# Doing the last layer's block endings inside its edge loop, at places given by limits

## The chip, the cores and the metric

One core of one Trainium2 chip. The metric is the device time of one execution in microseconds (us), median of several.

The engines go by their short names: in this kernel PE does the matrix products, DVE (vector engine) the sums and one-hots, ACT (scalar engine) the relu, POOL (GpSimd) issues the gathers, and SP issues plain loads and stores. SBUF and PSUM are the two memories in which the kernel has its tiles; the matrix products go to PSUM. A line of a timeline gives start and duration in us, engine, line of the kernel, operation, and what it writes and reads (out<-in); in brackets is the idle time of the engine before it and what ended that. A group line gives, behind its count (x), the busy time in us, the mean of one in ns, and the idle time before. The profile leaves numbers at the end of names out, so x3 is x there.

## The reference, cut to what matters

Four layers of a graph network on 4096 nodes of 512 features and 65536 edges, each added to its input. The last layer is a graph convolution with a linear map, a sum over edges and a relu:

```python
# layer 3; x is the result of layer 2 (the kernel calls it x3)
h = jnp.maximum(_layernorm(x, axis=-1), 0.0)
z = h @ W.T + b
out = jax.ops.segment_sum(norm[:, None] * z[row], col, num_segments=n)   # norm = dis[row] * dis[col]
x = x + jax.nn.relu(out)
```

`dst`, over which the last sum runs, is sorted and denser at low nodes (4096 u^2 with u uniform).

## The kernel before

The nodes are 32 blocks of 128. The edges are sorted by block and cut into tiles of 128; a block has a whole number of tiles, so that each tile adds to one block. The sums live in `acc`, 32 blocks of 128x512 in SBUF. The main part of the loop has 528 tiles; a branch holds up to 16 more, which these inputs do not need.

```python
def one_hots(pool, loc, t0, n):                         # which row of the block does each edge add to?
    oh = pool.tile([P, n, P], F32, name="oh")
    nc.vector.tensor_tensor(oh, row_i.unsqueeze(1).to_broadcast([P, n, P]),
                            loc[:, t0:t0 + n].unsqueeze(2).to_broadcast([P, n, P]), op=OP.is_equal)
    return oh

def add_to(b, ps):                                      # b is read from a table at run time
    into = acc[:, ds(b, 1), :D].rearrange("p b d -> p (b d)")
    nc.vector.tensor_add(into, into, ps)

# sum_edges: groups of U = 4 tiles, order of every engine fixed by hand
for i in range(-4, groups):
    if i + 4 < groups:
        g = got[i + 4] = ep.tile([P, U, D], F32, name="g", bufs=6)
        for j in range(U):
            gather(g[:, j, :], table, idx[:, t:t + 1])  # an indirect DMA, issued by POOL
    if 0 <= i + 1 < groups:
        ohs[i + 1] = one_hots(ep, loc, first + (i + 1) * U, U)
    # ... (nothing more for i < 0)
    for j in range(0, U, pair):
        # ... matmul of one-hots and gathered rows into PSUM
        add_to(block_of(nc.vector, bi, first + i * U + j), ps)

# ... layers 0 to 2, and the table ztab of layer 3 ...
in_two(1, TD_MAIN, TD, sum_edges(ztab, d_src, d_loc, bi_d, 1))     # main part, then a branch
with tc.tile_pool(name="l3_end", bufs=3) as lp:
    for b0 in range(0, NB, BG):                                    # BG = 4 blocks at a time
        xt = lp.tile([P, BG, D], F32, name="xt")
        nc.sync.dma_start(xt, blocks_of(x3, b0))
        for j in range(BG):
            b = b0 + j
            nc.scalar.activation(acc[:, b, :D], acc[:, b, :D], AF.Relu, scale=dis[:, b:b + 1])
            nc.vector.tensor_add(xt[:, j, :], xt[:, j, :], acc[:, b, :D])
        nc.sync.dma_start(blocks_of(out, b0), xt)
```

## Time and profile before

| | us |
|---|---|
| median, before | 6524.2 (6512.2 to 6527.4, 4 runs) |
| span of the profile | 6523.0 |
| last store of the table issued, to first gather of layer 3 | 3.95 |
| first to last gather of layer 3 | 661.0 |
| last gather to the end of the last sum | 5.9 |
| end of the last sum to the end of the program | 51.5 |

The table is read off the timeline. The prediction shows the lines that carry it. Three more are wanted, from the issue table of the kernel before: what goes where, from which queue, how many, how large, and the median time from issue to landing.

```profile
xt<-x SPq DMA_DIRECT2D x16, 1024.0 KB, 7.5
g<-ztab,d_src POOLq DMA_INDIRECT x528, 3.7
out_dram<-xt SPq DMA_DIRECT2D x8, 1024.0 KB, 4.9
```

### The profile page before, as it was taken

To read this page: it belongs to the slowest core of one execution; us is meant where nothing else is said; L and a number is where in the kernel's file an instruction comes from. 1 tells how busy PE (TensorE), PEld (TensorE's weight loads), DVE (VectorE), ACT (ScalarE), POOL (GpSimd) and SP (SyncE) were. 2 spreads that over 40 slices of the span, in tenths; PEclk is the share of its full clock that TensorE was granted. 3 is DMA by queue.
4 is the path that set the end of the run, shared out by engine and by line. 5 is a ranking of instruction groups with operands and counts; after the bars stand their busy time and mean duration, and the time that the engine had idled before them with its cause. 6 is when DMAs were issued, how large, how long until landed. Compare 5 with 4: busy or idle time off the path is not lost. (4 is left out here: it accounts for less than half of the span.)

```text
span 6523.0 us, 65629 instructions
## 1 busy us (share of the span) xinstructions
PE 5718.0 (88%) x18462; PEld 2778.4 (43%) x18462; DVE 4141.7 (63%) x7141; ACT 2937.3 (45%) x3977; POOL 3254.1 (50%) x3324
## 2 busy tenths in 40 slices
PE   6678887888779799999999999999999889978885
PEld 4366664322224344444444444444444365532221
DVE  7577778455443376676676776776766545556665
ACT  3244444300011277777777777777777533300001
POOL 1277772477760365555555555555555100037774
PEclk9899999999899899999999999999999899989998
DMA  8777775566774333333333333333333211137777
GB/s 225 182 220 214 218 215 176 162 201 203 195 214 175 125 109 103 102 98 104 101 98 105 101 98 102 103 98 106 100 98 104 82 45 62 59 106 209 210 209 243
DMA packets 399757, 926.39 MB, mean 142 GB/s; under 512 B 135926, under 2 KB 135926, under 8 KB 399382
## 3 DMA queue, kind: packets, MB, share of 16 engines
q0 software_dynamic: 230976, 721.66, 37.6%
q1 hardware_dynamic: 168406, 200.39, 9.6%
q8 instruction: 155, 2.54, 0.2%
q14 instruction: 220, 1.80, 0.1%
HBM read 818.71 MB, written 103.11 MB: 141 GB/s over the span
## 5 line engine op out<-in xcount | busy, mean ns | idle before, releaser
L438 PE MATMUL m_ps<-w_sb,h_t 128*128 128x512 f32 x4224 | 1905.9, 599 | 31.2 <-ACT h_t L957 31.2
L803 PE MATMUL sum_ps<-g,oh 128*128 128x512 f32 x2144 | 1146.9, 636 | 218.1 <-DMA g<-ztab,d_src 80.2
L438 PEld LDWEIGHTS m_ps<-w_sb,h_t 128*128 128x128 f32 x4224 | 771.1, 190 | 983.6 <-issue 791.2
L449 POOL DMA_INDIRECT qg<-qtab,eg x528 | 504.0, 954 | 990.6 <-ACT h_t L957 845.7
L449 POOL DMA_INDIRECT g<-ztab,d_src x528 | 501.4, 950 | 866.4 <-issue 811.6
L459 DVE TENSOR_TENSOR acc<-acc,sum_ps 128x512 f32 x800 | 550.2, 688 | 546.4 <-PE sum_ps L803 541.4
L803 PEld LDWEIGHTS sum_ps<-g,oh 128*128 128x128 f32 x2144 | 336.9, 191 | 1015.4 <-DVE acc L459 388.5
L449 POOL DMA_INDIRECT g<-ytab,s_dst x544 | 536.9, 987 | 353.2 <-DMA ytab<-acc 185.6
L914 POOL DMA_INDIRECT eg<-aug,d_eid x528 | 569.0, 1078 | 242.4 <-issue 131.0
L449 POOL DMA_INDIRECT rows<-htab,s_dst x544 | 585.9, 1077 | 204.9 <-issue 138.9
L957 ACT COPY h_t<-tr_ps 128x512 f32<-128x512 f32 x528 | 283.6, 589 | 777.6 <-PE tr_ps L955 777.6
L735 PE MATMUL sum_ps<-rows,oh 128*128 128x261 f32 x2176 | 551.5, 410 | 60.3 <-PE sum_ps L735 41.2
L449 POOL DMA_INDIRECT pg<-ptab,eg x528 | 508.7, 963 | 160.9 <-issue 160.6
L735 PEld LDWEIGHTS sum_ps<-rows,oh 128*128 128x128 f32 x2176 | 427.3, 202 | 163.3 <-PE sum_ps L735 66.3
L967 PE MATMUL small_ps<-z,oh 128*128 128x512 f32 x1056 | 477.8, 595 | 8.4 <-DVE z L1027 8.4
L1006 DVE TENSOR_TENSOR z<-m_ps,b_bc 128x512 f32<-128x512 f32 x132 | 91.3, 692 | 467.3 <-PE m_ps L438 467.3
L459 DVE TENSOR_TENSOR acc<-acc,small_ps 128x512 f32 x528 | 361.1, 684 | 31.8 <-PE small_ps L967 4.3
L1165 ACT ACTIVATE acc<-acc,dis 128x512 f32<-128x512 f32 x32 | 19.7, 706 | 671.2 <-DVEq L464 671.2
L1027 DVE TENSOR_TENSOR z<-z,t 128x1024 f32<-128x1024 f32 x264 | 310.4, 1217 | 8.2 <-ACTq L464 4.8
L992 DVE TENSOR_TENSOR z<-m_ps,b_bc 128x512 f32<-128x512 f32 x132 | 91.3, 692 | 352.6 <-PE m_ps L438 352.6
L967 PEld LDWEIGHTS small_ps<-z,oh 128*128 128x128 f32 x1056 | 201.5, 191 | 263.7 <-issue 221.9
L955 PEld LDWEIGHTS tr_ps<-ident,pg 128*128 128x128 f32 x2112 | 248.0, 142 | 151.1 <-issue 120.0
(248 smaller groups left out, 8389.5 us busy)
## 6 DMA issues: line engine op xcount, KB each, us to landing
aug<-row SPq DMA_DIRECT2D x32, 560.0 KB, 3.9
places<-loc_rows SPq DMA_DIRECT2D x68, 256.0 KB, 3.8
xt<-in_x_dram SPq DMA_DIRECT2D x16, 1024.0 KB, 5.7
row<-in_edge_attr_dram SPq DMA_DIRECT2D x32, 512.0 KB, 6.6
x<-xt SPq DMA_DIRECT2D x16, 1024.0 KB, 4.3
xt<-x SPq DMA_DIRECT2D x16, 1024.0 KB, 7.5
rows<-htab,s_dst POOLq DMA_INDIRECT x544, 3.8
g<-ytab,s_dst POOLq DMA_INDIRECT x544, 3.7
```

What stands on the lines that cost most here:

```text
L438: nc.tensor.matmul(ps, h_t[:, k, :], w_sb[:, k0 + k, :], start=start and k == 0, stop=stop and k == KC - 1)
L449: nc.gpsimd.indirect_dma_start(out=dst_ap, out_offset=None, in_=table, in_offset=bass.IndirectOffsetOnAxis(ap=idx, axis=0))
L459: nc.vector.tensor_add(into, into, ps)
L735: nc.tensor.matmul(ps[:, c, :HW], oh[:, j + k, :], rows[:, j + k, c * HW:(c + 1) * HW], start=k == 0, stop=k == 1)
L803: nc.tensor.matmul(ps, oh[:, j + k, :], g[:, j + k, :], start=k == 0, stop=k == pair - 1)
L914: nc.gpsimd.indirect_dma_start(out=eg[:, j // 2, (j % 2) * HALF:(j % 2 + 1) * HALF], out_offset=None, in_=aug.rearrange("e c -> (e c)").un ...
L955: nc.tensor.transpose(h_ps[:, k, :], h[:, j, k * P:(k + 1) * P], ident)
L957: nc.scalar.copy(h_t, h_ps)
L967: nc.tensor.matmul(ps, oh, m, start=True, stop=True)
L992: nc.vector.tensor_add(zz[:, 0, :], ps, b2_bc)
L1006: nc.vector.tensor_add(zz[:, 1, :], ps, b2_bc)
L1027: nc.vector.tensor_mul(mz[:, j:j + 2], mz[:, j:j + 2], t[:, j:j + 2])
```

## The change

Its intent is to take the ending off the end. Because the edges are sorted by block, a block's sums are complete long before the loop is. But where a block ends depends on the data, and the instruction order does not. So each block gets a limit, a tile after which it is taken to be complete: 230 + 10b for block b. A flag `late` is computed from the real ends; if a block ends behind its limit, a branch at the very end does all blocks over. ACT now writes to a tile of its own (`t_end`), not over `acc`, so that doing it over is possible.

```diff
+    LIMITS = ((32, 17), (230, 10))
 # ... in the sort, for each of the two orders o:
+        limit = pool.tile([1, NB], F32, name="limit")
+        nc.gpsimd.iota(limit, pattern=[[LIMITS[o][1], NB]], base=LIMITS[o][0], ...)
+        nc.vector.tensor_tensor(limit, til[:1, :], limit, op=OP.is_gt)
+        nc.vector.reduce_max(over, limit, axis=AX.X)
+        nc.vector.tensor_copy(late[:, o:o + 1], over)
 # ... in sum_edges, behind the four tiles of a group:
+                    if follow and first == 0:
+                        follow(first + (i + 1) * U)
 # ... the ending:
-    in_two(1, TD_MAIN, TD, sum_edges(ztab, d_src, d_loc, bi_d, 1))
-    with tc.tile_pool(name="l3_end", bufs=3) as lp:
-        # ... (the loop over blocks shown above)
+    class Ending:
+        def load(self, b):
+            if b < NB:
+                self.xs[b] = self.pool.tile([P, D], F32, name="x_end", bufs=self.ahead + 3)
+                nc.sync.dma_start(self.xs[b], x3[b * P:(b + 1) * P, :])
+        def follow(self, tiles):
+            self.finish()
+            while self.next < NB and tiles >= LIMITS[1][0] + LIMITS[1][1] * self.next:
+                self.begin()
+        def begin(self):
+            b, self.next = self.next, self.next + 1
+            t = self.pool.tile([P, D], F32, name="t_end", bufs=4)
+            nc.scalar.activation(t, acc[:, b, :D], AF.Relu, scale=dis[:, b:b + 1])
+            self.ready.append((b, t))
+        def finish(self):
+            for b, t in self.ready:
+                xt = self.xs.pop(b)
+                nc.vector.tensor_add(xt, xt, t)
+                nc.sync.dma_start(out[b * P:(b + 1) * P, :], xt)
+                self.load(b + self.ahead)
+            self.ready = []
+        # ... __init__ (six loads ahead), the_rest (what is left behind the loop)
+    with tc.tile_pool(name="l3_end", bufs=1) as lp:
+        ending = Ending(lp, 6)
+        sum_edges(ztab, d_src, d_loc, bi_d, 1, follow=ending.follow)(0, TD_MAIN)
+        ending.the_rest()
+    for flag in (more, late):
+        with tc.If(nc.values_load(flag[:, 1:2], min_val=0, max_val=1) > 0):
+            if flag is more:
+                sum_edges(ztab, d_src, d_loc, bi_d, 1)(TD_MAIN, TD)
+            with tc.tile_pool(name="l3_late", bufs=1) as lp:
+                Ending(lp, 6).the_rest()
```

More of the change, by code (lines that the diff above doesn't have):

```diff
@@ L97 @@
     more = keep_pool.tile([1, 2], I32, name="more")
+    late = keep_pool.tile([1, 2], I32, name="late")
     by_src = ctx.enter_context(ExitStack())
@@ L240, in by_order @@
         nc.vector.tensor_copy(more[:, o:o + 1], over)
+        limit = pool.tile([1, NB], F32, name="limit")
+        nc.gpsimd.iota(limit, pattern=[[LIMITS[o][1], NB]], base=LIMITS[o][0], channel_multiplier=0,
+                       allow_small_or_imprecise_dtypes=True)
+        nc.vector.tensor_tensor(limit, til[:1, :], limit, op=OP.is_gt)
+        nc.vector.reduce_max(over, limit, axis=AX.X)
+        nc.vector.tensor_copy(late[:, o:o + 1], over)
         tile_i = pool.tile([P, G], F32, name="tile_i")
@@ L773, with sum_edges @@
     l0_pool.close()
-    def sum_edges(table, idx, loc, bi, pair, beside=None):
+    def sum_edges(table, idx, loc, bi, pair, beside=None, follow=None):
         U = 4
@@ L1157, with __init__, the_rest @@
                     norm.rows(j, h3[p - 2][:, j, :], xt[:, j, :])
-    in_two(1, TD_MAIN, TD, sum_edges(ztab, d_src, d_loc, bi_d, 1))
-    with tc.tile_pool(name="l3_end", bufs=3) as lp:
-        for b0 in range(0, NB, BG):
-            xt = lp.tile([P, BG, D], F32, name="xt")
-            nc.sync.dma_start(xt, blocks_of(x3, b0))
-            for j in range(BG):
-                b = b0 + j
-                nc.scalar.activation(acc[:, b, :D], acc[:, b, :D], AF.Relu, scale=dis[:, b:b + 1])
-                nc.vector.tensor_add(xt[:, j, :], xt[:, j, :], acc[:, b, :D])
-            nc.sync.dma_start(blocks_of(out, b0), xt)
+    class Ending:
+        def __init__(self, pool, ahead):
+            self.pool, self.ahead, self.next, self.xs, self.ready = pool, ahead, 0, {}, []
+            for b in range(ahead):
+                self.load(b)
+        def load(self, b):
[18 more added lines that the diff above has]
+            self.ready = []
+        def the_rest(self):
+            self.finish()
+            while self.next < NB:
+                self.begin()
+                self.finish()
```

## The prediction

> **What bounds the kernel now.** The change touches only the last layer's loop over edges and what follows it, so I read that part. First the busy times by stretch (columns: stretch and its length, busy us and instruction counts of PE, weight loads, DVE, ACT, POOL, then granted clock, DMA share, GB/s). 5804 to 6466 is the loop, 6471 to 6523 the end.
>
> ```profile
> 5804.00:6178.00 374.00, 316.09 (x590) 89.96 (x590) 242.90 (x367) 0.00 (x0) 282.92 (x298) 0.99 0.71 208
> 6178.00:6466.00 288.00, 244.29 (x460) 70.59 (x460) 190.36 (x287) 0.00 (x0) 218.00 (x230) 0.99 0.71 210
> 6471.00:6523.00 52.00, 0.00 (x0) 0.00 (x0) 20.45 (x33) 19.70 (x32) 0.00 (x0) 0.52 0.90 323
> ```
>
> The loop uses 71% of the DMA engines, two thirds of DVE and none of ACT. The end uses the DMA engines at 90% and little else: two stretches with opposite limits, one behind the other. Next the chain that ended last: 0.319 of a window of 83 us is loads of x3 and 0.126 stores of the output.
>
> ```profile
> by line: DMA xt<-x 31.9%; DMA out_dram<-xt 12.6%; DVE xt L1166 8.3%; DVEq L1198 0.7%; issue 0.5%; SPq L1162 0.5%; DVEq L1166 0.2%
> ```
>
> Then the order in time where loop meets end, and at the last gather:
>
> ```profile
> 6465.57 0.95 POOL L449 DMA_INDIRECT g<-ztab,d_src  x1 [0.30 <-issue]
> ...
> 6470.78 0.69 DVE L459 TENSOR_TENSOR acc<-acc,sum_ps 128x512 f32 x1 [0.38 <-PE sum_ps L803]
> 6471.77 19.70 ACT L1165 ACTIVATE acc<-acc,dis 128x512 f32<-128x512 f32 x32 [671.21 <-DVEq L464]
> 6471.81 1.68 SPq L1162 DMA_DIRECT2D xt<-x  x3
> ...
> 6514.58 3.01 SPq L1167 DMA_DIRECT2D out_dram<-xt  x2
> ```
>
> The last sum ends at 6471.5 and the program at 6523.0: the end costs **51.5 us**, in which 8 MiB are loaded and 8 MiB stored, through three buffers. Last, who paces the loop: the groups of instructions of its steady part (5840 to 6466).
>
> ```profile
> L449 POOL DMA_INDIRECT g<-ztab,d_src x500 | 474.9, 950 | 152.3 <-issue 98.7 <-PE sum_ps L803 29.2 <-DMA g<-ztab,d_src 24.4
> L459 DVE TENSOR_TENSOR acc<-acc,sum_ps 128x512 f32 x500 | 343.8, 688 | 212.9 <-PE sum_ps L803 208.8 <-DVE acc L459 1.3
> L444 DVE TENSOR_TENSOR oh<-row_i,d_loc 128x512 f32<-128x512 f32 x124 | 84.9, 685 | 0.0
> ```
>
> POOL's idle time is 152.3 us before 500 gathers, 0.30 each, the same whatever it is put down to. So POOL runs without a stop, 0.95 + 0.30 = 1.25 us per gather, and 528 of them take 661 us (6465.57 - 5804.54). **Issuing the gathers is the bound**, PE and DVE follow. They land 3.7 us after issue, and a buffer of 24 tiles stands between, so small delays on PE or DVE are not felt by POOL.
>
> **What the Trainium skill says.** "Perfetto Trace Analysis", Optimization Strategy: where the contended engine changes over time, interleaving the regimes may help; the first fence is such a case. "DMA: Bandwidth & Descriptors", Issuing engines are not separate DMA queues: transfers of all issuers share the same 16 engines and interleave; so loads and stores put into the loop compete with the gathers, for which no run shows the price yet. "VectorE: DVE Perf Modes", The TRN2 errata: an fp32 add of N elements takes (N+151)/0.96 ns, 691 for 512; the trace has 687 to 688. "SBUF — State Buffer", SBUF: two separate sides: a DVE operation with two SBUF inputs shuts out a GpSimd operation that reads SBUF for its whole length. The trace agrees, and this matters here:
>
> ```profile
> 6195.64 0.68 DVE L444 TENSOR_TENSOR oh<-row_i,d_loc 128x512 f32<-128x512 f32 x1
> 6195.74 1.40 POOL L449 DMA_INDIRECT g<-ztab,d_src  x1 [0.30 <-issue]
> ...
> 6335.35 0.95 POOL L449 DMA_INDIRECT g<-ztab,d_src  x1 [0.30 <-DMA g<-ztab,d_src]
> 6335.86 0.69 DVE L444 TENSOR_TENSOR oh<-row_i,d_loc 128x512 f32<-128x512 f32 x1
> ```
>
> One-hots (two SBUF inputs) that run across a gather's start lengthen it: 1.40 instead of 0.95, about until the one-hots' end. The sums (one input in PSUM) start beside gathers all the time and lengthen none. In this loop one-hots mostly start 0.3 to 0.7 us after a gather starts, so they end before the next one, and only 8 of 528 gathers are over 1.0 us.
>
> **The change part by part.**
> 1. Removed: the end, 51.5 us.
> 2. Its work goes into the loop: block b is begun after tile 230 + 10b, rounded up to a group of 4. 520 is the last such number that is at most 528 (b = 29), so 30 blocks are done inside and two after. ACT has nothing else there. DVE gets 30 adds of 0.69 = 21 us in the 373 us of the last 298 tiles, where it idles a third, 125 us. ACT's read of a block holds back the next sum: in the layer before, such an ACT operation takes 0.72 and starts 0.04 after DVE; the one-hots (0.69) cover most of it. Nothing there reaches POOL through a buffer.
> 3. Are the limits kept? From the given edges I counted the tiles of each block: the last tile of every block lies 5 or more tiles within its limit (5 at blocks 19 to 24), the total is 527 of 528. So neither branch is taken and nothing is done twice.
> 4. Added end. After the last sum: ACT on block 30 (0.72), its add beside ACT on block 31, the second add, together about 2.2; a store of 256 KB, which lands in 2.0 to 2.5 in the issue table; about 1.5 for two branches and 0.9 for the closing of the program, as before. Sum **6.5 us**. Saved so far: 51.5 - 6.5 = 45.
> 5. Start of the loop. Nine loads of x3 now come beside the last store of ztab, which the first gather waits for (issued 5800.59, gather 5804.54). The order on the queue shows one load ahead of that store, eight just behind it: 2 MiB, some 6 us of the engines at the end's 323 GB/s. I charge **1.5**.
> 6. Shut-out. The order on DVE has each final add (two SBUF inputs) between a group's last sum and the one-hots after it. It takes the place of the one-hots, which is safe; but it pushes them back by 0.6, from 0.3-0.7 to 0.9-1.3 us of a 1.25 us cadence, that is, across the next gather's start. A lengthening of 0.2 to 0.45 then falls on POOL, the bound. 30 times 0.3 = **9 us** (an estimate from the fence above).
> 7. Limits: one iota and three DVE operations on 32 numbers in each of two sorts, some 0.15 us each: **0.7** at most.
>
> Sum: 45 - 1.5 - 9 - 0.7 = 34 us. From the median of 6524.5: **6490 us**, or 0.5% less.
>
> **Rivals.** (a) *Contention on the DMA engines sets the pace.* 55 transfers of 256 KB in 373 us are 39 GB/s. At the end's rate (0.90 for 323 GB/s) that is 0.11, and 0.71 becomes 0.82: room is left. Layer 0 speaks for it: a 256 KB load per 8 gathers, and gathers of 1077 ns on average. But there the long ones go with a DVE multiply of two SBUF inputs at the gather's start, and gathers beside the bulk of a load's packets have their 0.95. If it held all the same, 0.13 on 300 gathers would cost 39 us: the gain would be eaten, 6520. (b) *The adds shut out nothing*, since the phases shift or POOL has a reserve: 45 - 2 = 43 us, 6481. (c) *A block is late*, by a fault in my count: all 32 are redone behind the loop, 50 us or more: 6530 or above. (d) *DVE becomes the bound*: its share rises from 66% to about 72% in the second part, so no.
>
> **Range and chances.** (b) to a somewhat worse case of 6 gives 6478 to 6500; the three runs of before scatter by 15 us, so I widen to 6474 to 6506. 2% are 130 us, far more than the end that can be hidden, and more than any rival costs: within 2% with 0.98.
>
> **What would show it.** Right: the last sum to the end of the program 5 to 9 us; no instruction of either branch's body; POOL's gap before a gather still 0.30, but some 20 to 30 gathers of the last 298 at 1.1 to 1.45 us, each with one-hots across its start; loop from first to last gather 668 to 673 us; DMA share in the second part 0.80 to 0.84. Wrong: gathers lengthened where only loads or stores run (a), idle time of POOL above 0.30 (a buffer came late), fewer than 10 long gathers (b), or 32 more ACT operations after the loop (c). Any of these moves the time by its own term; the sign would turn only with (a) in full or (c).

## The result, and the profile after

6491.4 us (6483.5 to 6502.4, 4 runs) against 6524.2 us. The ratio is 0.9954, with a 95% interval from 0.9935 to 0.9974. (A ratio is the mean time of one kernel's fast runs over that of the other's of the same rounds, so not quite the ratio of the medians.) The change gains half a per cent. Executions over 1.5% slower than the fastest of the same kernel are left out of the means.

First the busy times by stretch of the changed kernel, with the columns of the prediction's first fence.

```profile
5803.00:6178.00 375.00, 310.64 (x586) 91.33 (x586) 244.44 (x371) 4.35 (x7) 284.62 (x297) 0.98 0.74 219
6178.00:6470.00 292.00, 231.62 (x453) 72.03 (x452) 201.46 (x306) 16.59 (x23) 223.40 (x225) 0.99 0.78 238
6470.00:6492.00 22.00, 9.48 (x19) 2.91 (x18) 9.30 (x14) 2.06 (x3) 5.83 (x6) 0.82 0.42 134
```

ACT now works inside the loop, and the DMA engines carry 238 GB/s where they carried 210. There are only 225 POOL operations in 292 us of the second stretch, that is 1.30 us each; before there were 230 in 288 us, 1.25 each. The loop has become slower. The end, from the timeline of the changed kernel:

```profile
6482.53 0.69 DVE L469 TENSOR_TENSOR acc<-acc,sum_ps 128x512 f32 x1 [1.60 <-PE sum_ps L813]
6483.31 1.33 ACT L1192 ACTIVATE t_end<-acc,dis 128x512 f32<-128x512 f32 x2 [10.22 <-DVE acc L469]
6484.07 1.30 DVE L1198 TENSOR_TENSOR x_end<-x_end,t_end 128x512 f32<-128x512 f32 x2 [0.85 <-ACT t_end L1192]
6484.78 0.94 SPq L1199 DMA_DIRECT2D out_dram<-x_end  x2
```

The last sum ends at 6483.2, two blocks are left, and the program ends at 6491.6: 8.4 us in place of 51.5. Where the time between went, by the same five stretches:

| stretch | before | after | difference |
|---|---|---|---|
| program start to the last store of the table | 5800.6 | 5798.0 | -2.6 |
| that store to the first gather | 3.95 | 4.81 | +0.9 |
| first to last gather | 661.0 | 673.7 | +12.7 |
| last gather to end of last sum | 5.9 | 6.7 | +0.8 |
| end of last sum to end of program | 51.5 | 8.4 | -43.1 |
| sum | 6523.0 | 6491.6 | -31.4 |

The first row is scatter: a second profile of each kernel, with nothing edited, had 5789.4 before and 5801.9 after (runs e10 and e11 below). Since the stages before the loop scatter by some 15 us (this row has 5787 to 5802 in the eleven profiles without an edit to layer 1, all but e7 and e9), more than what the experiments are about, I compare loops (first to last gather), and times only where the difference is larger.

The groups of instructions of the changed kernel, in the stretch from 6110 to 6460, in which endings run:

```profile
L459 POOL DMA_INDIRECT g<-ztab,d_src x271 | 268.8, 992 | 82.6 <-issue 71.6 <-DMA g<-ztab,d_src 5.8 <-PE sum_ps L813 5.2
L454 DVE TENSOR_TENSOR oh<-row_i,d_loc 128x512 f32<-128x512 f32 x67 | 46.0, 687 | 0.0
L1198 DVE TENSOR_TENSOR x_end<-x_end,t_end 128x512 f32<-128x512 f32 x27 | 18.6, 687 | 0.0
```

POOL's idle time is still 0.30 per gather (82.6 / 271). No buffer holds it up. The gathers themselves are longer, 992 ns on average where they had 950. Counted in the trace: of the last 298 gathers 44 are over 1.0 us (4 before), of the first 230 there are 6 (4 before). Each long one has one-hots or a final add across its start, as in this piece of the changed kernel's timeline:

```profile
6466.44 0.69 DVE L1198 TENSOR_TENSOR x_end<-x_end,t_end 128x512 f32<-128x512 f32 x1
6467.04 0.69 DVE L454 TENSOR_TENSOR oh<-row_i,d_loc 128x512 f32<-128x512 f32 x1
...
6467.27 1.27 POOL L459 DMA_INDIRECT g<-ztab,d_src  x1 [0.30 <-PE sum_ps L813]
```

The add takes the place of the one-hots, the one-hots slide to 6467.04, and the gather that starts at 6467.27 takes 1.27 us. It ends 0.81 us after the one-hots do; in the prediction's example the gather of 1.40 us ends 0.82 after them. Over the whole loop of the changed kernel 50 gathers are lengthened by over 0.05 us, 40 with one-hots and 10 with an add across their start, and every one ends 0.81 to 0.82 us after that operation does. One-hots that run only some 0.13 us or less into a gather lengthen nothing (0.95 = 0.13 + 0.82).

### The profile page after: what moved, and what is told of

It reads as the page before. It is cut to its first block, busy times and chain, and to the rows that moved or that the text cites. A ratio compares the mean times of both kernels' runs of the same rounds, so it can differ in the third digit from the quotient of the medians.

```text
span 6491.6 us, 65768 instructions
## 1 busy us (share of the span) xinstructions
PE 5700.9 (88%) x18462; PEld 2779.8 (43%) x18462; DVE 4140.9 (64%) x7147; ACT 2940.7 (45%) x3977; POOL 3264.9 (50%) x3326
## 5 line engine op out<-in xcount | busy, mean ns | idle before, releaser
L813 PE MATMUL sum_ps<-g,oh 128*128 128x512 f32 x2144 | 1133.7, 633 | 245.9 <-DMA g<-ztab,d_src 94.6
L1192 ACT ACTIVATE t_end<-acc,dis 128x512 f32<-128x512 f32 x32 | 23.0, 721 | 663.7 <-DVE acc L469 663.7
L979 PEld LDWEIGHTS small_ps<-z,oh 128*128 128x128 f32 x1056 | 201.5, 191 | 263.7 <-issue 221.9
```

The costliest lines, as they stand in the source:

```text
L813: nc.tensor.matmul(ps, oh[:, j + k, :], g[:, j + k, :], start=k == 0, stop=k == pair - 1)
L979: nc.tensor.matmul(ps, oh, m, start=True, stop=True)
```

## The experiments

**The theory** going in: the loop's 12.7 us are DVE operations with two SBUF inputs that run across the start of a gather and lengthen it (shut-out), because the final adds push the one-hots. **The rival**: the 16 MiB that now run on the DMA engines beside the gathers slow POOL or the gathers as such (contention). "Long" means over 1.0 us, counted among the last 298 gathers on the two digits that the timeline prints; e1, e8 and e10 have one more each if 1.002 to 1.005 us counts as long.

| run | loop, us | long | median, us (runs) |
|---|---|---|---|
| before; again (e10) | 661.0; 662.0 | 4; 6 | 6521.6 (8, the rounds of e6 to e8) |
| changed; again (e11) | 673.7; 672.9 | 44; 41 | 6491.4 (4, other rounds) |
| e1, adds in mid group | 667.5 | 23 | 6483.5 (4) |
| e2, transfers only | 670.9 | 35 | 6480.2 (4) |
| e3, ACT and adds only | 669.0 | 30 | 6487.1 (4) |
| e4, one-hots before the add | 672.6 | 46 | 6490.1 (4) |
| e5, ACT's result in PSUM | 668.4 | 24 | 6481.1 (1) |
| e6, and the one-hots' row | 658.8 | 0 | 6470.2 (4) |
| e7, combined version | 658.9 | 0 | 6458.7 (4) |
| e8, no branches | 672.4 | 42 | 6488.7 (4) |
| e9, kernel before with the row in PSUM | 658.7 | 0 | 6502.4 (4) |

In all of them but e6, e7 and e9 the first 230 gathers take 288.2 to 289.5 us, in those three 287.4 to 287.5: up to the first ending all loops with the same one-hots go alike.

### e1: the final adds in the middle of a group

```diff
                         side.step()
+                        if follow and first == 0 and j == 1:
+                            follow.__self__.finish()
                     if follow and first == 0:
                         follow(first + (i + 1) * U)
```

> Only the place of the final adds changes: after the second sum of a group instead of after its fourth. Shut-out theory: the add then lies 0.3 to 0.7 us after a gather's start, pushes no one-hots and crosses no gather's start. Of the last 298 gathers at most 12 are over 1.0 us (44 in the changed kernel), and first to last gather takes 661 to 664 us (673.7). Contention rival: transfers are the same, so 35 or more long gathers and 671 to 675 us.

Measured: 23 long gathers and 667.5 us. This lies between the two expectations: half of the loss goes, half stays. The place of the adds matters, with all transfers kept, which the rival cannot explain; but they are not all of it. Both expectations missed.

### e2: the transfers alone

```diff
-            t = self.pool.tile([P, D], F32, name="t_end", bufs=4)
-            nc.scalar.activation(t, acc[:, b, :D], AF.Relu, scale=dis[:, b:b + 1])
+            t = None
...
-                nc.vector.tensor_add(xt, xt, t)
+                nc.vector.memset(xt[:, 0:1], 0.0)
```

> The loads and stores of the ending stay in the loop, paced by a memset of one column on DVE; ACT operation and add are taken out (result wrong on purpose: x3 with a zeroed column). Shut-out theory: the memset has no SBUF input, so at most 15 of the last 298 gathers are over 1.0 us, loop 661 to 665 us. Contention rival: the transfers alone cost the 12 us, loop 671 to 675 us.

Measured (result wrong): 35 long gathers and 670.9 us. My theory missed here: with no add to push anything (the memset takes 0.06 us), most of the loss was there. The rival's range was met to 0.1 us. But every one of the long gathers again has one-hots across its start. What probably moved them shows in the waits of PE and in how long a gather takes to land, both from 6110 to 6460. The kernel before:

```profile
PE sum_ps L803 <- DMA g<-ztab,d_src: 45.2, 128, 2.0
DMA to landing us min/median/max: 3.4/3.6/5.5
```

Transfers only:

```profile
PE sum_ps L813 <- DMA g<-ztab,d_src: 65.0, 98, 1.6
DMA to landing us min/median/max: 3.5/4.2/5.6
```

The gathers land 0.6 us later in the median, and unevenly; PE waits 65 us for them, not 45. POOL keeps its own cadence, but sums and one-hots come behind the landings and slide against it. Counted from the trace over the last 72 one-hots of the loop: those that start less than 0.55 us before the next gather's start, so that they run over 0.13 us into it, are 6 in the kernel before, 34 in the changed one and 37 here (each to within 1, since the timeline has two digits). Starts at random in the cadence of 1.25 us would give 0.55 / 1.25 of 72, that is 32 (an estimate from these numbers): the kernel before has favourable places, the changed one and e2 about what chance gives. So I formed a second theory: *anything* that shifts DVE against POOL brings the shut-out, the pushing add and the late landing alike.

### e3: ACT and the adds alone

```diff
-            if b < NB:
+            if b >= self.ahead + 3 and b < NB:
+                self.xs[b] = self.xs[b - self.ahead - 3]
+            elif b < NB:
                 self.xs[b] = self.pool.tile([P, D], F32, name="x_end", bufs=self.ahead + 3)
...
-                nc.sync.dma_start(out[b * P:(b + 1) * P, :], xt)
+                if b >= NB - 2:
+                    nc.sync.dma_start(out[b * P:(b + 1) * P, :], xt)
```

> ACT operations and adds stay in the loop, loads beyond the first nine blocks and all stores but the last two are taken out (result wrong on purpose). Shut-out theory: 30 to 50 of the last 298 gathers over 1.0 us, loop 670 to 675 us as in the changed kernel. Contention rival: loop back at 661 to 664 us.

Measured (result wrong): 30 long gathers and 669.0 us, at the lower edge of the count and 1 us under the range of the theory, far from the rival's. Gathers land as before, in 3.7 us; 28 of 72 one-hots run across a start by the same count. So ACT and the adds alone cost 8 us and the transfers alone 10, and both together 12.7: not a sum, since a gather is lengthened once whatever moved the one-hots.

### e4: one-hots first, then the add

```diff
+                    if follow and first == 0 and i:
+                        follow(first + i * U)
                     g, oh = got.pop(i), ohs.pop(i)
...
-                    if follow and first == 0:
-                        follow(first + (i + 1) * U)
```

> The final add and the one-hots change places on DVE: one-hots first, the add behind them. Shut-out theory: the second of the two operations is the one that crosses a gather's start, whichever it is; so the count stays at 30 to 50 long gathers in the last 298 and the loop at 670 to 675 us, but now most long ones have the add across their start (10 of 50 in the changed kernel). A rival that only one-hots hurt: under 12 long gathers and 661 to 664 us.

Measured: 46 long gathers and 672.6 us, as expected of the theory; but of the 55 gathers of the whole loop that are lengthened by over 0.05 us only 15 have the add across their start, 41 the one-hots (one has both). The part of the expectation on which of the two it would be was wrong. That fits the second theory: the landings move the one-hots in any order.

### e5 and e6: nothing with two SBUF inputs

In e5 ACT writes `t_end` into PSUM; the add keeps its place and length. In e6 the row that the one-hots compare with is copied into PSUM once, too, before the loop.

```diff
+            self.tpool = pool                      # e5 and e6; then set to a pool in PSUM
-            t = self.pool.tile([P, D], F32, name="t_end", bufs=4)
+            t = self.tpool.tile([P, D], F32, name="t_end", bufs=2)
...
+                row = None                         # e6 alone
+                if follow:
+                    row = rps.tile([P, P], F32, name="row_ps")      # rps: a pool in PSUM
+                    nc.vector.tensor_copy(row, row_i)
-                        ohs[i + 1] = one_hots(ep, loc, first + (i + 1) * U, U)
+                        ohs[i + 1] = one_hots(ep, loc, first + (i + 1) * U, U, row)
```

> ACT writes its result into PSUM, so the final add has one SBUF input; its place and length are unchanged, and it still pushes the one-hots. Shut-out theory: the long gathers with the add across their start (10, 4.1 us in the changed kernel) vanish, those with the one-hots (40, 10.1 us) stay: loop 668 to 672 us. Rival that the adds themselves are the cost: 661 to 663 us. Contention rival: unchanged, 673 to 675 us.

> As the run before, and the row of numbers that the one-hots compare with lies in PSUM too, so no DVE operation of this loop has two SBUF inputs. Shut-out theory: no gather over 1.0 us at all in this loop, first to last 659 to 661.5 us, under the kernel before change (661.0). Contention rival: 35 or more long gathers in the last 298, 671 to 675 us.

Measured in e5: 668.4 us; no lengthened gather is left that has the add alone across its start, and in the whole loop 32 with one-hots remain (one of them has the add across its start too). As expected. In e6 none is long and the loop takes 658.8 us, 2 us less than before the change and 0.2 under the expected range. The groups of instructions of e6, then its gathers (shortest, median and longest in ns) and their landing, all from 6110 to 6460:

```profile
L459 POOL DMA_INDIRECT g<-ztab,d_src x277 | 261.9, 945 | 84.4 <-issue 69.8 <-DMA g<-ztab,d_src 7.9 <-PE sum_ps L818 6.7
L454 DVE TENSOR_TENSOR oh<-row_ps,d_loc 128x512 f32<-128x512 f32 x69 | 47.2, 684 | 0.0
L1204 DVE TENSOR_TENSOR x_end<-x_end,t_end 128x512 f32<-128x512 f32 x28 | 19.0, 680 | 0.0
```

```profile
L459 POOL DMA_INDIRECT g<-ztab,d_src x277: 942/946/955, 6109.1 to 6454.1; - x139
DMA to landing us min/median/max: 3.5/4.1/5.6
```

This is the run that decides. Transfers, ACT and adds are all there; gathers land as late as in e2 (4.1); 32 of 72 one-hots run across a gather's start, about as in the changed kernel. Only the place of one input of each operation is different, and the longest gather is 955 ns. With the same one-hots and no ending in it, the loop takes 658.7 (e9 below). So transfers cost nothing by themselves here, and neither do adds; the shut-out is the whole of the 12.7 us, and of the kernel before's few long gathers as well. That the late landings are what moved the one-hots in e2 rests on the views above; I did not vary the landing by itself.

### e7: the combined version

e1 and e6 together, and the row in PSUM in layer 1's edge loop as well (`if first == 0` in place of `if follow`).

> Both in this loop (adds in mid group and PSUM), and one-hots from PSUM in layer 1's edge loop as well, where 74 of 549 indirect issues were lengthened by 23 us in all, 20 us of it with one-hots across their start. Shut-out theory: layer 3's loop 659 to 661.5 us, layer 1's loop shorter by 15 to 22 us, the program 28 to 38 us faster than the changed kernel: 6453 to 6464 us. Contention rival: about as the changed kernel, 6485 to 6495 us.

Measured: 6458.7 us (6457.6 to 6459.9), ratio to the kernel before 0.9903 (0.9886 to 0.9919), correct; within the expectation, but for the loop of layer 3 (0.1 us under its range). Layer 1's loop goes from 710.6 to 691.4 us (705.4 to 711.2 in the eleven profiles that leave it alone). Its gathers from 1220 to 1900, first in the kernel before, then here:

```profile
L449 POOL DMA_INDIRECT g<-ytab,s_dst x520 | 514.2, 989 | 160.7 <-issue 109.4 <-DMA g<-ytab,s_dst 27.8 <-PE sum_ps L803 23.4
```

```profile
L459 POOL DMA_INDIRECT g<-ytab,s_dst x535 | 507.8, 949 | 166.5 <-issue 109.1 <-DMA g<-ytab,s_dst 28.9 <-PE sum_ps L818 28.2
```

Fifteen more gathers fit into the same stretch. In that whole loop 10 gathers are still over 1.0 us (75 in the kernel before); none has one-hots across its start, all have another DVE operation with two SBUF inputs there, of the sort that runs beside this loop, and all end 0.81 to 0.83 us after it. This is the version that beats both.

### e8: without the branches

```diff
-    for flag in (more, late):
-        with tc.If(nc.values_load(flag[:, 1:2], min_val=0, max_val=1) > 0):
-            # ... (both bodies)
```

> The two branches behind the loop are left out (these inputs take neither). Last sum to end of program is 8.4 us in the changed kernel, of which my 6.5 had 1.5 for the branches. If the branches wait for the last store to land and add their time behind it: 5.5 to 6.5 us. If they run beside the store: 8 to 8.5 us as now. The loop itself is unchanged, 672 to 675 us.

Measured: last sum to end 5.6 us in the profile (6485.1 to 6490.7), so two branches that are not taken cost 2.8 us. The waits of the DMA queue after 6483 in the changed kernel help to say how (L1214 is the line of the branches):

```profile
SPq L1199 <- DVE x_end L1198: 6.9, 2, 6.7
SPq L1214 <- SPq L1214: 3.0, 3, 1.5
```

The queue waits 3.0 us at the branches, 2.6 of them until the two last stores have landed (6487.28 and 6488.40), and DVE reads the second flag only at 6488.7, 3.3 us after the last add. The branches stand in line behind the stores, not beside them. In e8 the queue waits for the same landings, so this wait is not the price. Issue of the last store to its landing is 3.0 us in the changed kernel and 2.1 in e8; its landing to the end of the program is 3.2 and 1.35, since the second branch and its semaphores come before the closing of the program. The first part costs 0.9, the second 1.8. Both repeat within 0.1 us in the other kernels with branches that end with an add and a store; why the store lands later is not shown. (This kernel is right for these inputs only.)

### e9: the kernel before with the row in PSUM

The edit of e6 to the one-hots, in layers 1 and 3, applied to the kernel before the change.

> The kernel before the change, with the row that the one-hots compare with in PSUM in the edge loops of layers 1 and 3, and nothing else. Shut-out theory: layer 1's loop shorter by 18 to 21 us as in the last combined version (711 to 691), layer 3's by 2 (661.0 to 659); the program at 6521.6 - 21 = 6500 us, 6494 to 6506. Then the change itself is worth 38 to 44 us where nothing is shut out (against 6458.7 of the combined version), instead of 31. Rival, that the combined version's gain over the changed kernel comes from elsewhere: 6515 us or more here.

Measured: 6502.4 us (6497.9 to 6503.0), 2 us above the middle of the expectation; loops of 690.9 and 658.7 us. Against e7 (another round of runs, in which the kernel before had 6521.6, here 6520.7) the ending in the loop is worth 6502.4 - 6458.7 = 43.7 us: all of the 43.1 that the end lost. In the change as made, over a quarter of that is given back in the loop.

### e10 and e11: both kernels again

> A second profile of the kernel before, to see how far one repeats: loop of layer 3 661 us within 1, at most 6 long gathers in its last 298, last sum to end 51 to 52 us. The stage before the loop ended between 5787 and 5801 us in eight profiles so far; here anywhere in that range if that is scatter, at 5799 to 5802 if the unchanged part got faster with the change.

> A second profile of the changed kernel: loop 671 to 675 us, 38 to 48 long gathers in the last 298, last sum to end 8 to 8.5 us. The end of the stage before the loop as in the run above: scatter between 5787 and 5801 us.

Measured: 662.0 and 672.9 us, 6 and 41 long gathers, last sum to end 51.7 and 8.3 us. The loops repeat within 1 us. The stage before the loop ended at 5789.4 and 5801.9, this time the other way round, so it is scatter.

## Why the prediction was right

Time and direction were right: 6490 predicted, 6491.4 measured, and 34 us of gain predicted where the medians have 32.8 and the profiles 31.4 with 2.6 of scatter in the change's favour (28.8 without). By its steps:

1. **The end removed, 51.5.** Held: nothing of it is left but two blocks.
2. **Work that hides in the loop.** Held: POOL's idle time stayed 0.30, and the second part's share of DVE is 201.5 / 292 = 69% (72 predicted). The last sums came 0.8 us later behind the last gather, which had no term.
3. **No block late.** Held: ACT has as many operations as before (3977), so neither body ran.
4. **Added end, 6.5.** It was 8.4. The terms as written add up to 6.6 to 7.1, not 6.5. The one that was too small is the branches: 1.5 was put down, e8 measured 2.8, of which 0.9 shows as a later landing of the last store (3.0 us, where 2.0 to 2.5 was put down).
5. **Start of the loop, 1.5.** 0.9 in the profile, 1.2 in the second one (5801.90 to 5807.06, against 3.95 in both of before).
6. **Shut-out, 9.** The loop lost 12.7 (10.9 between the second profiles). The lengthening of one gather, 0.3, was right (13.5 us over 44 of them); their number was not, 44 in place of 20 to 30. The step named the pushing adds alone. e2 showed that the transfers do the same, about as often as ACT and the adds do (e3), most likely through later landings. Its reading that one-hots "end before the next one" holds for most, not for all: in the kernel before, too, 26 of the last 72 run across a gather's start, but 20 of them by so little that it lengthens nothing.
7. **The limits, 0.7.** As written it is 1.2 (eight operations of 0.15). In the trace they take 0.14 to 0.18 each. What they cost in time is not separable from the scatter of the stages before; open.

Steps 4 and 6 were too small by 1.9 and 3.7, step 5 too large by 0.6; a scatter of 2.6 came to meet them. So a part of the closeness is luck.

**The rivals.** (a), contention: its time in e2 looked like it, but e6 has the same transfers and no loss; what the transfers cost they cost through the shut-out. The sign that the prediction gave for (a), long gathers where only transfers run, was badly chosen: e2 showed just that, and needed the one-hots at each start to be read right. (b), no shut-out at all: refuted by 44 long gathers, and it is what e6 then made. (c), a late block: did not happen. (d), DVE as the bound: POOL's gaps did not change.

**The signs.** Last sum to end 5 to 9: 8.4. Loop 668 to 673: 673.7, just outside. DMA share 0.80 to 0.84: 0.78, since the estimate kept the gathers' rate and they slowed down.

## What to carry to other kernels

When a tail is moved into a loop that one engine paces, price not only busy shares but what the new work does to that engine's own instructions: look in the trace for its longest ones and for what stood at their start. Phases that happen to be harmless in a steady loop are not kept when transfers or a few operations are added, so take away the cause (here one input moved to PSUM) rather than tune the order: moving the adds brought back half, moving the inputs all of it and 2 us more. And a branch behind the last stores is part of the tail even when it is not taken.

## What the Trainium skill lacked or had wrong

- "SBUF — State Buffer", SBUF: two separate sides, says that whichever of the two starts first has the shared port for its whole instruction. For DVE the traces agree: a gather that it holds up ends 0.81 to 0.82 us after the DVE operation (up to 1.47 us in all, in e8, in place of 0.95). For the gather they do not: only its start holds up DVE. In the changed kernel's loop seven one-hots or adds that start within 0.03 us of a gather's start take 0.70 to 0.75 us in place of 0.68 to 0.69, and those gathers keep their 0.95; one-hots that start 0.1 to 0.9 us after a gather's start, while it still runs, have their usual length.
- "DMA: Bandwidth & Descriptors", Issuing engines are not separate DMA queues, says that transfers interleave, without a price. Here gathers land in 3.9 to 4.2 us in the median with the ending's loads and stores beside them, and in 3.6 to 3.7 without; a store of 256 KB lands in 3.8 in the loop, and in 2.0 to 2.5 in stages without gathers.
- "Advanced Engine Details and Errata", Control Flow Timing, times a branch by itself; no page that was found has what one that is not taken costs behind outstanding stores: 2.8 us for two (last sum to end 8.4 us with them, 5.6 without).
